# Sixteen third steps instead of twelve: four more quarter products split by Strassen-Winograd, and the vector work around them reordered

## The chip, the cores and the metric

The kernel runs on one core of a Trainium2 chip. The metric is the device time of one execution in microseconds (us); the median of several runs is given. A profiled execution of the kernel before gives a trace: instructions of each engine with start and duration, the semaphore waits between them, and the DMA transfers. Engines are named as in the profile: PE (TensorE matmuls), PEld (its weight loads), DVE (VectorE), ACT (ScalarE), POOL (GpSimd) and SP (SyncE). A name such as L463 is line 463 of the kernel.

## The reference

Two layers act on `x` of 8 sequences x 256 tokens x 1024 features, in fp32. The first adds a dense product and a gated LoRA term; the second adds a product with one of 16 whole weight matrices, chosen per sequence.

```python
def layer0(x, language_ids, W, Wr, A, B):        # W 1024x1024, 8 experts of rank 16
    base = jnp.einsum('btd,od->bto', x, W)
    logits = jnp.einsum('btd,ed->bte', x, Wr)
    logits = logits + (one_hot(language_ids, 8) * 5.0)[:, None, :]
    topw, topi = jax.lax.top_k(logits, 2)
    weights = softmax(topw)
    gates = jnp.sum(one_hot(topi, 8) * weights[..., None], axis=-2)
    h = jnp.einsum('btd,erd->bter', x, A)
    return base + 2.0 * jnp.einsum('bter,bte,eor->bto', h, gates, B)

def layer1(x, adapter_ids, weight):              # weight 16x1024x1024
    return jnp.einsum('bsi,boi->bso', x, weight[adapter_ids])

x = x + layer0(x, itok_B_0_7, W, Wr, A, B)
x = x + layer1(x, itok_B_0_15, weight)
```

## The kernel before, in words

**The first layer** is one 1024 x 1024 x 2048 product, done by Strassen-Winograd steps. The identity is added to W's diagonal (`add_identity`), so that the residual comes with the product. The first step cuts weights, inputs and outputs in two each way: blocks `w11` to `w22`, `x11` to `x22`, `y11` to `y22`. It leaves seven block products, called 1, 2, 5, 6, 3, 7 and 4 in the order in which they run. Product 1 is written out in `opening`; the others are calls of `product`. Sums of blocks that a product needs are made by VectorE (`w_sum`: S1, S2, S3, S4) or by DMAs that add to what they find (`add_x`, `add_raw` on POOL's queue, after plain loads by `raw` on SP's).

**The second step** cuts each block product into seven leaves of 256 x 256 x 512: `make_subs` makes the sums s1 to s4 of weights and t1 to t4 of inputs. In the profile's names a leaf adds into a PSUM pair A, X or B; `roles` hands the three pairs round from product to product. A plain leaf is four matmuls with a 512-wide moving operand (`mm`, L551). A matmul in fp32 stands in the trace as two records, and in the products `up` and `hg` add the LoRA rows as further matmuls.

**The third step** cuts a leaf again, into seven pieces of 128 x 128 x 256. `third` gives the eight small sums (r1 to r4 of weights, 128 wide, and q1 to q4 of inputs, 256 wide), `piece(n)` the matmul of piece n (L463), and `take(n)` its eviction. Pieces 1, 6 and 7 add into one bank one after another, with an eviction in between; piece 5 has a bank of its own; pieces 2, 3 and 4 add into the leaf's pair. So piece 6 waits for the evictions of piece 1, and piece 7 for those of piece 6. In the kernel before, twelve leaves have a third step: leaves 3 and 4 of product 1 (in `opening`), leaf 2 of products 2, 5, 6, 3, 7 and 4, leaves 3 and 4 of product 5, and leaf 4 of products 3 and 4.

**The order of VectorE's work** is set by a small planner while the program is written out. `queue` holds pending operations, each with a cost, the events it needs and a key; `now` counts estimated PE and DVE time. `ahead` writes out queued operations that are free before TensorE's time, `force(key)` writes out what a matmul is about to need, and `after` an eviction. `us(n)` is the cost of an operation on n elements. `opening` is written out by hand.

**The gates**: `project` multiplies x by A and Wr together (136 columns a token tile, L256), `take(j, c)` splits logits from h, `gating(j)` makes the top-2 gates with some twenty small operations on VectorE and multiplies them onto h, and `turn(j, banks)` transposes h on TensorE (L326), from where ScalarE copies it to `hg`. j is the half of the tokens.

**The second layer** (`adapt`, matmuls at L863, the last at L930) takes one sequence at a time with one Winograd step; `load_w1` brings its weights, `prep_w1` and `prep_y` make its sums.

Of the kernel before, what the change touches and what calls it, by code (L numbers as in the profile page):

```python
# [25 lines left out]
def kernel(  # L26
# [31 lines left out]
    nc = tc.nc  # L58
# [171 lines left out]
    def add(out_, x, y):  # L230
        tt(out_, x, y, ALU.add)
# [58 lines left out]
    def gating(j):  # L290
# [29 lines left out]
        ]  # L320
        return [(0.23, f) for f in ops] + [(1.22, onto_h)]

# [24 lines left out]
    queue = []  # L347
    done = {}

    def us(n):  # L350
        return (n + 151) / 960

    def vec(t, fn, key=None):
        fn()
        now["dve"] += t
        done[key] = now["dve"]

# [7 lines left out]
    def ahead(until):  # L365

        while now["dve"] < until:
            may = [(t, i) for i, t in enumerate(map(free, queue)) if t is not None and t < until]
            ready = [i for t, i in may if t <= now["dve"]]
            if ready:  # L370
                t, _, key, fn = queue.pop(ready[0])
                vec(t, fn, key)
            elif may:
                now["dve"] = min(may)[0]
            else:
                return
# [35 lines left out]
    def third(key, leaf, lhs, rhs, place, what):  # L412
# [10 lines left out]
        def op(name, tag, fn, x, y, what):  # L423
            width = P if name[0] == "r" else NQ

            def run():
                if place == 0:
                    t[name] = sub3.tile([P, width], F32, name=f"{name}_{key}{leaf}", tag=tag)
                else:
# [18 lines left out]

        def piece(n, acc=None, banks=None):
            if n in (1, 5):  # L450
# [11 lines left out]
            }[n]()  # L462
            nc.tensor.matmul(out_, lhsT=l, rhs=r, start=(n in (1, 5)), stop=True, skip_group_check=True)  # L463
            now["pe"] += 0.432
# [13 lines left out]

    def make_subs(key, w, x, leaves=(), what=(), last=(), place=0):

# [58 lines left out]
    def multiply(up=None, tokens=None):  # L539


        def mm(acc, lhs, rhs, first=False, rows=None, c=0, part=(0, 1), ms=(0, 1), need=()):
            if rows == "d":
                force("bdiff")
            for key in need:
# [17 lines left out]
    def opening(key, dest):  # L563
# [23 lines left out]
        for f in sums_of[:4]:  # L587
            f()
        add(dest[:, 0], A, dest[:, 0])
        wide = pair("ids_wide", 0)[:, 0, :NB]  # L590
        nc.tensor.matmul(wide, lhsT=ones, rhs=ids_f[:, :NB], start=True, stop=True)
# [8 lines left out]
        event(f"{key}:P6")  # L600
        project(0, 0, None, range(KH, KC), False)
        take(0, 0)

        late[0][3]()
        ops, ops3, piece, out = third(key, 3, lambda: t["s2"], lambda: b(1, 1), 0, ())
        for o in ops:
            vec(o[0], o[3], o[2])
        late[1][3]()
        mm(A, t["s3"], t["t3"])
# [3 lines left out]
        q1, q2 = dest[:, 1], dest[:, 2]  # L613
        chunk(0)
# [6 lines left out]
        piece(6)  # L621
        out(6, q1, q1)
        chunk(2)
        for n in (2, 3, 4):
# [4 lines left out]
        last_out = out  # L629
        ops, ops3, piece, out = third(key, 4, lambda: a(1, 1), lambda: t["t2"], 0, ())  # L630
        for o in ops[:2]:
            vec(o[0], o[3], o[2])
        last_out(5, q1, q1)
        for o in ops[2:]:
            vec(o[0], o[3], o[2])
        add(q1, B, q1)
        chunk(4)
        piece(1)
        out(1, q2)
        chunk(5)  # L640
        piece(5)
# [8 lines left out]
        piece(7)  # L650
        out(7, q2)
        out(5, q2, q2)
        add(q2, A, q2)

    def product(key, base, dest, lora=None, tokens=None, sub=False, joined=None):

# [61 lines left out]
        if 4 in deep:  # L718
            _, _, piece4, take4 = deep[4]
            piece4(1)  # L720
            take4(1, at[2], old[2], sub)
        if 3 in deep:
            _, _, piece, take = deep[3]
            force(f"{key}.X2")
# [12 lines left out]
            for n in (2, 3, 4):  # L737
                piece(n, B)
            if 4 in deep:
                force(f"{key}.A7")  # L740
                mm(A, None, None, False, "1", 0, part=())
            piece(7)
            take(7, at[1], at[1], sub)
            take(5, at[1], at[1], sub)
        else:
# [3 lines left out]
        if 4 in deep:  # L749
            if 3 not in deep:  # L750
                piece4(5)
                piece4(6)
                take4(6, at[2], old[2], sub)
                force(f"{key}.A7")
                mm(A, None, None, False, "1", 0, part=())
# [9 lines left out]
        join(2)  # L765
        ahead(now["pe"])


# [218 lines left out]
    done.clear()  # L987
    now["pe"], now["dve"] = 0.0, 3.5
    after(0.4, lambda: take(0, 1))
# [3 lines left out]
    now["pe"] += 7.5  # L993
    subs2 = make_subs("2", "12", "21", (2,))
    run(subs2[:2])
# [15 lines left out]
    gates = queue[-1][2]  # L1011
    queue += [(0.69, (), "I22", lambda: add_identity(wb["22"]))]
    queue += w_sum(minus, "21", "22", "21", (), "S1")
    queue += [(2.0, (), "bdiff", b_differences)]
# [4 lines left out]
    now["pe"] += 2.0  # L1019
# [8 lines left out]
    queue += w_sum(minus, "12", "11", "12", (), "S4")  # L1028
    queue += make_subs("3", "12", "12", (2, 4), ("x22",), "6", 1)
# [10 lines left out]
    queue += [(t, ("w0",), f"w0_{i}", f) for i, (t, _, f) in enumerate(prep_w1(0, 0))]  # L1040
    y0 = []
# [4 lines left out]

    queue += [(0.69, ("4:P7", "7:join2"), f"y0_{i}", lambda i=i: prep_y0(i)) for i in range(4)]
# [60 lines left out]
```

## Time and profile before

| what | value |
|---|---|
| median of 3 runs | 426.36 us (425.69 to 426.7) |
| the profiled execution's own time | 425.69 us |
| its span, first to last instruction | 423.7 us |
| PE, DVE, ACT busy | 418.8, 287.6, 40.6 us |
| first matmul of the opening, of product 2, of the second layer | 4.17, 59.25, 227.75 us |
| granted TensorE clock, mean | 1.00 |
| DMA traffic | 72.61 MB, mean 171 GB/s |

The span leaves out 2.0 us that lie around it in the device time. Matmuls overlap in the trace, so a matmul's cost in the queue is read from the starts of neighbours, not from its own duration: a 512-wide record lasts 592 ns and the next starts after 429. The same holds for VectorE: an operation on 1024 elements lasts 1.22 us and the next can start after 1.13. A group of rows merged in the timeline has the start of the first and the time to the end of the last.

### The profile page before, as it was taken

What the parts mean: (1) busy time and instruction counts of PE and PEld (TensorE: products, weight loads), DVE (VectorE), ACT (ScalarE), POOL (GpSimd) and SP (SyncE); (2) the same over time, 40 slices, a digit from 0 to 9 for tenths busy, and PEclk for the clock granted to TensorE, in tenths of its full rate; (3) what the DMA queues carried; (4) which work ended last, traced back from release to release, by engine and by line L of the source; (5) the groups of instructions that cost most, each with busy time, mean ns of one, the idle gap of its engine ahead of it and who ended that gap; (6) DMA issues with size and microseconds to landing.
All of it is one profiled execution on the core that took longest, in us unless ns stands there. A gap on an engine that the chain in (4) does not pass through costs nothing.

```text
span 423.7 us, 3569 instructions
## 1 busy us (share of the span) xinstructions
PE 418.8 (99%) x1294; PEld 226.1 (53%) x1294; DVE 287.6 (68%) x439; ACT 40.6 (10%) x69; POOL 17.6 (4%) x26
## 2 busy tenths in 40 slices
PE   8999999999999999999999999999999999999996
PEld 6579975445655454554555444444444444444574
DVE  1645699957888989878786666765747666665531
ACT  2010120022110000000000101010101101010110
POOL 1000020110001101103000000000000000000000
PEclk9999999999999999999999999999999999999999
DMA  8995089476220964918902384666658385650202
GB/s 274 385 397 236 2 173 210 126 184 101 100 99 4 179 215 78 294 24 155 342 0 99 116 321 159 242 214 213 224 194 300 109 298 190 213 183 0 101 0 99
DMA packets 20257, 72.61 MB, mean 171 GB/s; under 512 B 1552, under 2 KB 3856, under 8 KB 15248
## 3 DMA queue, kind: packets, MB, share of 16 engines
q1 hardware_dynamic: 15088, 58.87, 38.0%
q0 software_dynamic: 3904, 12.58, 16.6%
q10 hardware_dynamic: 1248, 0.93, 0.7%
q8 instruction: 10, 0.16, 0.1%
q14 instruction: 7, 0.06, 0.0%
HBM read 55.61 MB, written 8.39 MB: 151 GB/s over the span
## 4 chain that ended last, share of the span: by engine, by line
PE 99%; POOL 0%; ACT 0%; issue 0%; POOLq 0%
PE A L863 23%; PE A L551 21%; PE B L551 13%; PE B L863 13%; PE ps_h L256 7%; PE X L863 6%; PE P L463 5%; PE A_last L930 3%; PE X L551 3%; PE X L463 2%; PE A L463 1%; PE idle L568 1%; PE B L463 1%; PE ps_g L326 0%; ACT z L960 0%
## 5 line engine op out<-in xcount | busy, mean ns | idle before, releaser
L551 PE MATMUL A<-t,s 128*128 128x512 f32 x112 | 50.3, 592 | 0.0
L863 PE MATMUL B<-x,x 128*128 128x512 f32 x96 | 43.2, 592 | 0.0
L863 PE MATMUL A<-w,x 128*128 128x512 f32 x88 | 39.6, 592 | 0.0
L228 DVE TENSOR_TENSOR w<-w,w 128x1024 f32<-128x1024 f32 x24 | 29.1, 1223 | 15.1 <-PE A L863 15.1
L863 PE MATMUL A<-w,y 128*128 128x512 f32 x88 | 39.1, 592 | 0.0
L256 PEld LDWEIGHTS ps_h<-y,x 128*128 128x128 f32 x256 | 31.7, 190 | 3.3 <-issue 2.9
L551 PEld LDWEIGHTS A<-t,s 128*128 128x128 f32 x112 | 21.2, 190 | 21.2 <-issue 20.6
L256 PE MATMUL ps_h<-y,x 128*128 128x136 f32 x256 | 31.9, 279 | 0.0
L863 PEld LDWEIGHTS B<-x,x 128*128 128x128 f32 x96 | 18.2, 190 | 22.1 <-issue 22.0
L863 PEld LDWEIGHTS A<-w,x 128*128 128x128 f32 x88 | 16.7, 190 | 21.0 <-issue 21.0
L863 PEld LDWEIGHTS A<-w,y 128*128 128x128 f32 x88 | 16.7, 190 | 20.6 <-issue 20.6
L228 DVE TENSOR_TENSOR y<-P,y 128x512 f32<-128x512 f32 (+1 forms) x31 | 17.6, 567 | 14.0 <-PE P L463 9.1
L228 DVE TENSOR_TENSOR y<-A,y 128x1024 f32<-128x1024 f32 x17 | 20.8, 1223 | 8.3 <-issue 4.6
L551 PE MATMUL A<-x,w 128*128 128x512 f32 x56 | 25.4, 594 | 0.0
L551 PE MATMUL B<-x,s 128*128 128x512 f32 x40 | 18.0, 592 | 0.0
L228 DVE TENSOR_TENSOR x<-w,x 128x1024 f32<-128x1024 f32 (+1 forms) x11 | 10.6, 968 | 10.8 <-PE A L863 7.8
L225 ACT ACTIVATE z<-A 128x512 f32<-128x512 f32 x12 | 7.2, 597 | 101.4 <-PE A L863 101.4
L228 DVE TENSOR_TENSOR w<-x,w 128x1024 f32<-128x1024 f32 x8 | 9.7, 1225 | 10.2 <-PE A L863 5.7
L551 PEld LDWEIGHTS A<-x,w 128*128 128x128 f32 x56 | 10.3, 190 | 10.8 <-issue 10.5
L228 DVE TENSOR_TENSOR z<-z,X 128x512 f32<-128x512 f32 x7 | 4.8, 687 | 15.9 <-PE X L863 15.9
L551 PE MATMUL B<-t,s 128*128 128x512 f32 x32 | 15.0, 595 | 0.0
L863 PE MATMUL X<-w,y 128*128 128x512 f32 x32 | 14.4, 592 | 0.0
(179 smaller groups left out, 555.8 us busy)
## 6 DMA issues: line engine op xcount, KB each, us to landing
x<-w_dram SPq DMA_DIRECT2D x24, 1024.0 KB, 5.1
x<-xT_dram SPq DMA_DIRECT2D x10, 1024.0 KB, 10.6
w<-w_dram SPq DMA_DIRECT2D x8, 1024.0 KB, 4.8
out_dram<-z SPq DMA_DIRECT2D x15, 512.0 KB, 3.0
x<-x POOLq DMA_DIRECT2D x4, 1024.0 KB, 9.9
x<-xT_dram POOLq DMA_DIRECT2D x4, 1024.0 KB, 9.3
y<-y POOLq DMA_DIRECT2D x8, 512.0 KB, 5.3
w<-wT_dram SPq DMA_DIRECT2D x3, 1024.0 KB, 15.3
```

What stands on the lines that cost most here:

```text
L225: nc.scalar.activation(out_, x, AF.Copy, scale=scale)
L228: nc.vector.tensor_tensor(out_, x, y, op)
L256: nc.tensor.matmul(ps[v][:, u * EA : (u + 1) * EA], lhsT=xk(k, j, c)[:, ts(r, P)], rhs=aw_sb[:, k, :], start=(first and k == some[0] and u ...
L463: nc.tensor.matmul(out_, lhsT=l, rhs=r, start=(n in (1, 5)), stop=True, skip_group_check=True)
L551: nc.tensor.matmul(acc[:, m, :], lhsT=l, rhs=r, start=(first and i < len(ms)), stop=(i >= len(steps) - len(ms)), skip_group_check=True,)
L568: nc.tensor.matmul(idle[:, 0, :P], lhsT=ident, rhs=ident, start=True, stop=True)
L863: nc.tensor.matmul(accs[name], lhsT=lhs[:, k // 2, k % 2, :], rhs=rhs[:, k, :], start=(first and k == 0), stop=(k == KH - 1), skip_group_c ...
L930: nc.tensor.matmul(acc, lhsT=lhs[:, k // 2, k % 2, :], rhs=rhs[:, k, ts(v, m)], start=(first and k == 0), stop=(k == KH - 1), skip_group_c ...
```

## The change

Four more leaves get a third step: leaf 5 of product 1, leaf 4 of products 2 and 6, and leaf 3 of product 4.

- In `opening` the leaf s1 x t1 is cut. Its result is needed in two quarters of y21, q3 and q1. ScalarE copies pieces 1, 6 and 7 into both (`both`), VectorE adds piece 5 to both, and pieces 2 to 4 (P3's sums) are held in B. B is added to q3, then leaf 3's pieces 2 to 4 are added into B as well, and B is added to q1. `add_B` leaves out the quarter that no piece writes. A after s2 x t2, copied by ScalarE before, is added to q1 by VectorE. The sums of leaves 3 and 4 are made one leaf earlier, and some go into free space of y12 (`place == 3`).
- w22's identity, the weight sum S1 and the differences of B's rows (`b_differences`) move from the planner's queue in product 2 to the end of the opening.
- The second half's transposes move from after product 2 to within it (`between=turn_1`), into pair X.
- In `product`, leaf 4's pieces 5 and 6 stand between the halves of B where leaf 3 is not cut; where it is, leaf 3's last piece and evictions come before A's LoRA rows. While leaves 3 and 4 are under way, `hold` keeps the planner to operations whose key begins with the product's number.
- S4 enters the queue before product 5 and no longer before product 3. The planner's costs change. At the start of the second layer pairs X and B swap roles.

The diff, cut to its core:

```diff
     def us(n):
-        return (n + 151) / 960
+        return (n + 66) / 960
     def vec(t, fn, key=None):
         fn()
         now["dve"] += t
-        done[key] = now["dve"]
+        done[key] = now["dve"] + 0.1
     def ahead(until):
         while now["dve"] < until:
-            may = [(t, i) for i, t in enumerate(map(free, queue)) if t is not None and t < until]
+            may = [
+                (t, i)
+                for i, t in enumerate(map(free, queue))
+                if t is not None and t < until and queue[i][2][0] in (hold[0] or queue[i][2][0])
+            ]
...
         if 4 in leaves:
-            deep[4] = third(key, 4, lambda: a(1, 1), lambda: t["t2"], 2, (f"{key}:P6",))
+            deep[4] = third(key, 4, lambda: a(1, 1), lambda: t["t2"], 3 if early else 2, (f"{key}:P6",))
...
     def opening(key, dest):
...
         for f in sums_of[:4]:
             f()
+        ops, ops3, piece, out = third(key, 5, lambda: t["s1"], lambda: t["t1"], 0, ())
+        for o in ops[:2]:
+            vec(o[0], o[3], o[2])
         add(dest[:, 0], A, dest[:, 0])
...
+        own = halves(pair(f"P5_{key}", 0))
         B = pair(f"B_{key}", 2)
-        mm(B, t["s1"], t["t1"], True)
-        nc.scalar.copy(dest[:, 3], B)
+        def both(n):
+            out(n, q3)
+            out(n, q1)
+        def add_B(q):
+            for m, n in ((0, 2 * NQ), (1, NQ)):
+                add(q[:, m, :n], B[:, m, :n], q[:, m, :n])
+        piece(1, banks=own)
+        piece(5, banks=own)
+        both(1)
+        mm(A, t["s2"], t["t2"])
...
+        piece(6)
+        both(6)
+        for n in (2, 3, 4):
+            piece(n, B, fresh=True)
+        project(0, 0, None, (KH,), False, False)
+        piece(7)
+        both(7)
+        add(q1, A, q1)
+        for q in (q3, q1):
+            out(5, q, q)
+        add_B(q3)
+        project(0, 0, None, range(KH + 1, KC), False)
+        take(0, 0)
-        mm(A, t["s2"], t["t2"])
-        nc.scalar.copy(dest[:, 1], A)
...
         piece(7)
         out(7, q2)
+        add_identity(wb["22"])
+        for f in w_sum(minus, "21", "22", "21"):
+            f[3]()
+        b_differences()
         out(5, q2, q2)
         add(q2, A, q2)
...
-    def product(key, base, dest, lora=None, tokens=None, sub=False, joined=None):
+    def product(key, base, dest, lora=None, tokens=None, sub=False, joined=None, between=None):
...
+        if between is not None:
+            between(X)
         if 3 in deep:
+            hold[0] = key
...
+        elif 4 in deep:
+            mm(B, t["s2"], b(1, 1), False, "d", 1, ms=(0,), need=K("s4", "B5"))
+            piece4(5)
+            mm(B, t["s2"], b(1, 1), False, "d", 1, ms=(1,))
+            piece4(6)
+            take4(6, at[2], old[2], sub)
...
-    subs2 = make_subs("2", "12", "21", (2,))
+    subs2 = make_subs("2", "12", "21", (2, 4), early=True)
...
-    product("2", y21, y11, 0, 0)
-    force(gates)
-    turn(1, singles("ps_g_1"))
+    def turn_1(X):
+        force(gates)
+        turn(1, halves(X))
+        now["pe"] += 1.8
+    product("2", y21, y11, 0, 0, between=turn_1)
...
-    queue += make_subs("6", "11", "22", (2,), ("T2",), "5", 0)
+    queue += make_subs("6", "11", "22", (2, 4), ("T2",), "5", 0)
+    queue += w_sum(minus, "12", "11", "12", (), "S4")
     product("5", None, y22, 1, 1)
...
-    queue += make_subs("4", "22", "22", (2, 4), ("T4",), "7", 1)
+    queue += make_subs("4", "22", "22", (2, 3, 4), ("T4",), "7", 1)
...
+    role[1:] = role[2], role[1]
     for u in range(NB):
```

More of the change, by code (lines that the diff above doesn't have):

```diff
@@ L320, in gating @@
         ]
-        return [(0.23, f) for f in ops] + [(1.22, onto_h)]
+        return [(0.26, f) for f in ops] + [(us(2 * TQ), onto_h)]
     def turn(j, banks):
@@ L348 @@
     done = {}
+    hold = [""]
     def us(n):
-        return (n + 151) / 960
+        return (n + 66) / 960
     def vec(t, fn, key=None):
@@ L428, in run @@
                     t[name] = sub3.tile([P, width], F32, name=f"{name}_{key}{leaf}", tag=tag)
+                elif place == 3:
+                    t[name] = flat(yb["12"])[:, 2048 + at[tag] : 2048 + at[tag] + width]
                 else:
@@ L447, in third, with piece @@
         ]
-        def piece(n, acc=None, banks=None):
+        def piece(n, acc=None, banks=None, fresh=False):
             if n in (1, 5):
@@ L462, in piece @@
             }[n]()
-            nc.tensor.matmul(out_, lhsT=l, rhs=r, start=(n in (1, 5)), stop=True, skip_group_check=True)
+            nc.tensor.matmul(out_, lhsT=l, rhs=r, start=(n in (1, 5) or fresh and n in (2, 4)), stop=True, skip_group_check=True)
             now["pe"] += 0.432
@@ L477, in third, with make_subs @@
         return ops, ops3, piece, take
-    def make_subs(key, w, x, leaves=(), what=(), last=(), place=0):
+    def make_subs(key, w, x, leaves=(), what=(), last=(), place=0, early=False):
         before = (f"{last}:P7",) if last else ()
@@ L542, in mm @@
         def mm(acc, lhs, rhs, first=False, rows=None, c=0, part=(0, 1), ms=(0, 1), need=()):
-            if rows == "d":
-                force("bdiff")
             for key in need:
@@ L588, in opening @@
             f()
+        q1, q2, q3 = (dest[:, q] for q in (1, 2, 3))
+        ops, ops3, piece, out = third(key, 5, lambda: t["s1"], lambda: t["t1"], 0, ())
+        for o in ops[:2]:
+            vec(o[0], o[3], o[2])
         add(dest[:, 0], A, dest[:, 0])
-        wide = pair("ids_wide", 0)[:, 0, :NB]
+        wide = pair("ids_wide", 2)[:, 0, :NB]
         nc.tensor.matmul(wide, lhsT=ones, rhs=ids_f[:, :NB], start=True, stop=True)
         use_ids(wide)
+        own = halves(pair(f"P5_{key}", 0))
         B = pair(f"B_{key}", 2)
-        mm(B, t["s1"], t["t1"], True)
-        nc.scalar.copy(dest[:, 3], B)
+        def both(n):
[8 more added lines that the diff above has]
+        mm(A, t["s2"], t["t2"])
+        event(f"{key}:P6")
+        for o in ops[2:]:
+            vec(o[0], o[3], o[2])
         for f in sums_of[4:]:
             f()
-        mm(A, t["s2"], t["t2"])
-        nc.scalar.copy(dest[:, 1], A)
-        event(f"{key}:P6")
-        project(0, 0, None, range(KH, KC), False)
-        take(0, 0)
+        for o in ops3:
+            vec(o[0], o[3], o[2])
         late[0][3]()
-        ops, ops3, piece, out = third(key, 3, lambda: t["s2"], lambda: b(1, 1), 0, ())
-        for o in ops:
+        next_leaf = third(key, 3, lambda: t["s2"], lambda: b(1, 1), 3, ())
+        for o in next_leaf[0]:
             vec(o[0], o[3], o[2])
         late[1][3]()
+        piece(6)
[11 more added lines that the diff above has]
+        take(0, 0)
+        ops, ops3, piece, out = next_leaf
         mm(A, t["s3"], t["t3"])
@@ L612, in opening @@
         chunk = lambda k: project(0, 1, quarter, (k,), k == 0, k == KC - 1)
-        q1, q2 = dest[:, 1], dest[:, 2]
         chunk(0)
@@ L622, in opening @@
         out(6, q1, q1)
+        next_leaf = third(key, 4, lambda: a(1, 1), lambda: t["t2"], 0, ())
+        for o in next_leaf[0]:
+            vec(o[0], o[3], o[2])
         chunk(2)
@@ L629, in opening @@
         last_out = out
-        ops, ops3, piece, out = third(key, 4, lambda: a(1, 1), lambda: t["t2"], 0, ())
-        for o in ops[:2]:
-            vec(o[0], o[3], o[2])
+        ops, ops3, piece, out = next_leaf
         last_out(5, q1, q1)
-        for o in ops[2:]:
-            vec(o[0], o[3], o[2])
-        add(q1, B, q1)
+        add_B(q1)
         chunk(4)
+        chunk(5)
         piece(1)
         out(1, q2)
-        chunk(5)
         piece(5)
@@ L738, in product @@
                 piece(n, B)
+            piece(7)
+            take(7, at[1], at[1], sub)
+            take(5, at[1], at[1], sub)
             if 4 in deep:
@@ L741, in product @@
                 mm(A, None, None, False, "1", 0, part=())
-            piece(7)
-            take(7, at[1], at[1], sub)
-            take(5, at[1], at[1], sub)
+        elif 4 in deep:
[4 more added lines that the diff above has]
+            take4(6, at[2], old[2], sub)
         else:
@@ L750, in product @@
             if 3 not in deep:
-                piece4(5)
-                piece4(6)
-                take4(6, at[2], old[2], sub)
                 force(f"{key}.A7")
@@ L765, in product @@
         join(2)
+        hold[0] = ""
         ahead(now["pe"])
@@ L987 @@
     done.clear()
-    now["pe"], now["dve"] = 0.0, 3.5
+    now["pe"], now["dve"] = 0.0, 6.0
     after(0.4, lambda: take(0, 1))
@@ L1011 @@
     gates = queue[-1][2]
-    queue += [(0.69, (), "I22", lambda: add_identity(wb["22"]))]
-    queue += w_sum(minus, "21", "22", "21", (), "S1")
-    queue += [(2.0, (), "bdiff", b_differences)]
     queue += make_subs("5", "21", "12", (2, 3, 4), ("T1",), "2", 1)
-    product("2", y21, y11, 0, 0)
-    force(gates)
-    turn(1, singles("ps_g_1"))
-    now["pe"] += 2.0
+    def turn_1(X):
[3 more added lines that the diff above has]
+    product("2", y21, y11, 0, 0, between=turn_1)
     raw("21", 0, 1)
@@ L1027 @@
     event("x22", 14.0)
-    queue += w_sum(minus, "12", "11", "12", (), "S4")
     queue += make_subs("3", "12", "12", (2, 4), ("x22",), "6", 1)
@@ L1037 @@
     event("w0", 18.0)
-    queue += make_subs("4", "22", "22", (2, 4), ("T4",), "7", 1)
+    queue += make_subs("4", "22", "22", (2, 3, 4), ("T4",), "7", 1)
     product("7", y21, y21, joined=(y22, y21))
-    queue += [(t, ("w0",), f"w0_{i}", f) for i, (t, _, f) in enumerate(prep_w1(0, 0))]
+    queue += [(t, ("w0",), f"4.w{i}", f) for i, (t, _, f) in enumerate(prep_w1(0, 0))]
     y0 = []
@@ L1045, in prep_y0 @@
         y0[i][2]()
-    queue += [(0.69, ("4:P7", "7:join2"), f"y0_{i}", lambda i=i: prep_y0(i)) for i in range(4)]
+    queue += [(0.6, ("4:P7", "7:join2"), f"4.y{i}", lambda i=i: prep_y0(i)) for i in range(4)]
     product("4", y21, y21, 1, 0)
```

## The prediction

> **What bounds the kernel now.** I read the page's span and busy rows first, then its chain, then what TensorE waited for, then busy times by stage, then timelines around the edits.
>
> ```profile
> span 423.7 us, 3569 instructions
> PE 418.8 (99%) x1294; PEld 226.1 (53%) x1294; DVE 287.6 (68%) x439; ACT 40.6 (10%) x69; POOL 17.6 (4%) x26
> PE 99%; POOL 0%; ACT 0%; issue 0%; POOLq 0%
> ```
>
> TensorE is busy from 1.4 us to the end, and the chain that ended last is TensorE alone. Its only recorded wait is at the start:
>
> ```profile
> PE idle L568 <- POOL ident masks.py:199: 1.4, 1, 1.4
> ```
>
> So whatever is taken from TensorE's queue shortens the span one for one, as long as no operand or bank comes late. The stage view says where that could happen (columns: stretch, its length, then busy time of PE, PEld, DVE, ACT, POOL, the clock, DMA):
>
> ```profile
> 15.90:30.00 14.10, 14.10 (x58) 8.36 (x58) 5.62 (x15) 2.77 (x4) 0.00 (x0) 1.00 1.06 392
> 59.20:89.90 30.70, 30.70 (x82) 14.98 (x81) 27.97 (x56) 2.92 (x6) 3.00 (x3) 1.00 0.86 181
> 120.30:144.10 23.80, 23.80 (x64) 11.96 (x64) 21.22 (x26) 1.58 (x2) 2.56 (x2) 1.00 0.32 49
> 144.10:174.20 30.10, 30.10 (x86) 15.98 (x85) 26.27 (x44) 1.00 (x1) 2.61 (x3) 1.00 0.68 177
> 198.00:227.90 29.90, 29.90 (x85) 15.92 (x84) 22.57 (x34) 1.00 (x1) 0.86 (x1) 1.00 0.56 176
> ```
>
> These are the opening's middle, and products 2, 6, 3 and 4. TensorE fills each. VectorE has 8.5 us free in the first and 2.7, 2.6, 3.8 and 7.3 us in the others: it is the engine that more work could turn into a bound.
>
> **What the Trainium skill says.** "TensorE: Matmul & The Clock Gate", Step-by-step: what each phase is for, says that weights are loaded ahead of matmuls still in flight. The trace agrees: 226 us of loads, no idle TensorE. It also shows the exception, a bank that comes free just as its turn comes:
>
> ```profile
> 36.70 1.09 PE L256 MATMUL ps_h<-y,x 128*128 128x136 f32 x8
> 37.65 0.70 PE L463 MATMUL P<-t,w 128*128 128x256 f32 x2
> 38.18 1.09 PE L256 MATMUL ps_h<-y,x 128*128 128x136 f32 x8
> ```
>
> VectorE's last read of that bank (36.90 plus 0.69) ended at 37.59. The two records took 0.53 us to the next start; elsewhere 0.43. So a just-in-time release costs 0.10 us without showing as idle. "VectorE: DVE Perf Modes", The perf-mode tier table (the rule you actually need), lists a two-tensor fp32 operation at 1× alone, from SBUF or PSUM; the trace agrees, with starts 1.135 us apart for 1024 elements, 0.60 for 512, 0.34 for 256 and 0.205 for 128. I use these steps below.
>
> **The change part by part.** *Four leaves get a third step*: P5 of the first product (opening), leaf 4 of products 2 and 6, leaf 3 of product 4. A leaf was four 512-wide matmuls, eight records of 0.429 us: 3.43 us (A at 120.28 to 123.78, less its 0.07 of late release). Split, it is seven 256-wide ones, 14 records of 0.216: 3.02 us (three in a row started at 34.05, 34.48, 34.91). The changed program's order confirms the count: 372 matmuls of 512 for 388, 144 of 256 for 116. TensorE: 4 x (3.02 - 3.43) = **-1.63 us**, all on the path.
>
> *VectorE pays.* Each leaf needs four 128-wide and four 256-wide sums, 4 x 0.205 + 4 x 0.34 = 2.18 us, and in a product four more evictions, 2 x 0.34 + 2 x 0.60 = 1.88: 4.06 us in each of products 2, 6 and 4. In the opening there are 2.18 of sums, 1.13 for A (ScalarE copied it), 2 x 0.60 for P5's halves, 0.94 for the held sums into q3, and 0.2 saved on q1: 5.3 us. ScalarE there swaps two 1.01 us copies for four of 0.37 and two of 0.59. None is on the path if each leaf's operands are early. I laid the changed order of each queue out with the durations above; four places come within 0.3 us:
>
> (a) *Opening, A for P6.* The sum y<-A must have read A before t2·s2 is added. Before, P5's 3.43 us stood between; now only pieces 1 and 5.
>
> ```profile
> 13.68 1.22 DVE L228 TENSOR_TENSOR t<-x,t 128x1024 f32<-128x1024 f32 x1
> 14.82 1.22 DVE L228 TENSOR_TENSOR y<-A,y 128x1024 f32<-128x1024 f32 x1
> ```
>
> ```profile
> 15.55 0.38 PE L591 MATMUL ids_wide<-ids_f,ones 1*128 1x8 f32 x2
> 15.86 3.70 PE L551 MATMUL B<-t,s 128*128 128x512 f32 x8
> ```
>
> VectorE now does r1 and q1 first: y<-A from 14.82 + 0.55 = 15.37 to 16.59. TensorE arrives at 15.86 + 0.86 = 16.72: 0.13 us to spare. (b) *Opening, A for P7.* TensorE: 16.72, A 3.43, piece 6 0.43, pieces 2 to 4 1.29, one chunk 0.93, piece 7 0.43, three chunks 2.78: at 26.0. Piece 7's result is there at 23.4; two ScalarE copies (the pair at 59.45 took 1.07) to 24.5, y<-A to 25.75: 0.25 to spare. (c) *Product 6, piece 7 of leaf 4.* From the end of P7: TensorE needs 1, half of B, 5, half of B, 6, 2 to 4, that is 6 x 0.43 + 2 x 1.72 = 6.02 us. VectorE: r1, q1 0.5, A7 1.13, P1 0.34, four sums 1.09, product 3's s 0.60, r3 and q3 0.55, its t 1.13, then P6's eviction to 5.8: 0.2 to spare. (d) *Product 4, leaf 3's piece 5*: A7 and two evictions of P1 end 2.4 us after P7; TensorE has 0.43 + 0.43 + 1.72 = 2.58: 0.2 to spare. Each costs 0 to 0.10 us when met as at 37.65, and what it is late when late. I take 0.15 for all, less the just-in-time releases of before, 0.10 at 37.65 and 0.07 at 120.28, whose order changes: -0.02, ends -0.17 and +0.8.
>
> *Moves that I cost at nothing.* The second gates' eight transposes (0.87 us, at 89.74 before) now stand within product 2, in bank X: the same count; their gates ended at 66.9, X is read out at 79.5, and ScalarE's two copies (1.1 us) have until the first use at 96.20. w22's identity, S1 and the b differences (0.60 + 2 x 1.135 + 1.6 = 4.5 us) leave product 2, which makes room for its 4.06, and go into the opening's hole, where VectorE waited 2.90 us for ScalarE until 44.37. They wait for w21, which landed at 39.6 (issued 22.3, 17.3 to landing), some 0.7 us ahead; behind them stand leaf 4's last evictions and the second half's gating, whose banks TensorE needs near 50: some 5 us of cover. S4 (2.3 us) moves from product 3 (148.46) into products 5 and 6: that makes room for what product 6 pushes out. SP's second x21 load (83.07) waits some 3 us longer for leaf 4's operands, and the load and POOL's add behind it with it; product 7 first reads them near 174. The planner's changed costs, the hold, and the swapped banks of the second layer only order the queues; no PSUM bank is added.
>
> Sum: -1.63 - 0.02, about **-1.6 us**. Against the profiled execution's own 425.69 us (span 423.7 and 2.0 around it) that gives 424.1. The median shown is 426.36, 0.67 above; I carry the difference over: 424.8. About 0.2% (0.85 us) is what a measurement of this kernel can tell from no change.
>
> **Rivals.**
> 1. *The gain is given back in waits (no change).* The places (a) to (d) miss: 0.2 to 0.5 us each, about 1.2 in all, -0.4 net: 426.0. For: spare times of 0.13 to 0.25 us. Against: they are differences of rows that repeat within 0.01 us. Chance 0.12.
> 2. *VectorE becomes the bound in products 6 and 3 (slower).* From 120.3 to 174.2 it was busy 47.5 of 53.9 us; with 4.06 more and S4's 2.3 gone it has 49.3, 91%. If chained small sums run longer than those of before, or TensorE's evictions queue behind them, product 3's s and t, which in my layout are 0.7 us early at its B (147.84 before), come late, and each product behind inherits it. It decides from 0.7 us of added VectorE delay on; at the whole 4.06 less 0.7, 3.4 us is lost: 428.1. Against: after product 7, VectorE has 4.0 us free. Chance 0.08.
> 3. *It doesn't do what it says*: 256-wide pieces cost over half a 512. The rows exclude it (0.432 against 0.858), and it is in the sum.
>
> **How the numbers follow.** My forecast, 424.8 us, chance 0.80: faster by over 0.2%. Rival 1 gives within 0.2% (0.12), rival 2 slower (0.08). The range starts 0.8 below, for the runs' scatter (425.69 to 426.7), and reaches to 426.4, taking in the bound of +0.8 and rival 1; rival 2 is left out.
>
> **What would show each step.** After: PE busy near 417.2, 1318 records, the chain still TensorE alone; seven P and B starts 0.43 apart in the opening where B took 3.70; A at 16.7 and 26.0 with no idle before it; product 2's first A at 58.8 instead of 59.25; the second layer's first matmul near 226.1 instead of 227.75; VectorE near 305 us. Wrong: TensorE idle named <-DVE at A in the opening or at B or P in products 6, 3, 4, or a second layer that starts later than 227.

## The result, and the profile after

The changed kernel takes **424.38 us** (median of 20 runs, 423.75 to 425.23), the kernel before, run beside it, 426.01 us (20 runs, 425.08 to 426.74). The ratio is 0.9964, with a 95% interval of 0.9958 to 0.9970: 1.63 us or 0.36% less, beyond the 0.2% that the prediction took as the least that can be told from no change. The forecast was 424.8 us.

The page of the profile after, its span, its busy times and its chain:

```profile
span 422.2 us, 3674 instructions
PE 417.1 (99%) x1318; PEld 230.7 (55%) x1318; DVE 304.8 (72%) x489; ACT 40.9 (10%) x73; POOL 17.6 (4%) x26
PE 99%; POOL 0%; ACT 0%; issue 0%; POOLq 0%
```

TensorE has 24 records more (1318 for 1294) and is busy 1.7 us less; VectorE is busy 17.2 us more; the chain is still TensorE alone. In the waits of TensorE there is again only the start:

```profile
PE idle L573 <- POOL ident masks.py:199: 1.4, 1, 1.4
```

The stages that the prediction showed, in the windows of the profile after (same columns: stretch, its length, then PE, PEld, DVE, ACT, POOL, clock, DMA), in the order opening, product 2, product 6, product 3, product 4:

```profile
15.90:30.00 14.10, 14.10 (x67) 9.88 (x67) 11.65 (x27) 3.01 (x8) 0.00 (x0) 1.00 1.06 391
...
58.80:89.50 30.70, 30.70 (x93) 16.59 (x92) 26.61 (x59) 4.01 (x8) 3.00 (x3) 1.00 0.87 184
...
119.30:142.40 23.10, 23.10 (x69) 12.84 (x68) 21.37 (x36) 1.58 (x2) 2.56 (x2) 1.00 0.27 50
142.40:172.60 30.20, 30.20 (x86) 16.06 (x86) 30.06 (x51) 1.00 (x1) 2.34 (x3) 1.00 0.67 169
...
196.20:226.10 29.90, 29.90 (x92) 17.18 (x91) 26.74 (x46) 1.00 (x1) 0.89 (x2) 1.00 0.58 178
```

TensorE fills every stretch. The surprise is the fourth line: in product 3 VectorE is busy 30.06 of 30.20 us, 99.5%, and yet TensorE doesn't wait.

**A finer ruler.** The time to the `ids_wide` row in the opening differs by up to 1.25 us between profiled executions (it starts between 15.29 and 16.54 us). Behind it the traces repeat closely: three executions of kernels without a late TensorE (the one above, e9 and e11 below) agree within 0.01 us. So from here on kernels are compared by their *length*: from the start of `ids_wide` to the end of the last matmul. Before: 15.55 to 420.26, **404.71 us**. After: 15.65 to 418.53, **402.88 us**. That is 1.83 us less. The medians show 1.63 of it; where the rest may lie is said at the end, under the median.

### The profile page after: what moved, and what is told of

The parts are those of the page before. It is cut to its first block, busy times and chain, and to the rows that moved or that the text cites. A ratio compares the mean times of both kernels' runs of the same rounds, so it can differ in the third digit from the quotient of the medians.

```text
span 422.2 us, 3674 instructions
## 1 busy us (share of the span) xinstructions
PE 417.1 (99%) x1318; PEld 230.7 (55%) x1318; DVE 304.8 (72%) x489; ACT 40.9 (10%) x73; POOL 17.6 (4%) x26
## 4 chain that ended last, share of the span: by engine, by line
PE 99%; POOL 0%; ACT 0%; issue 0%; POOLq 0%
PE A L908 23%; PE A L556 20%; PE B L908 13%; PE B L556 11%; PE ps_h L256 7%; PE X L908 7%; PE P L470 6%; PE A_last L975 3%; PE X L470 3%; PE X L556 3%; PE A L470 2%; PE B L470 1%; PE idle L573 1%; PE X L326 0%; PE ps_g L326 0%; ACT z L1005 0%
## 5 line engine op out<-in xcount | busy, mean ns | idle before, releaser
L228 DVE TENSOR_TENSOR y<-A,y 128x1024 f32<-128x1024 f32 x18 | 22.0, 1222 | 9.3 <-PE A L556 5.8
L228 DVE TENSOR_TENSOR y<-P,y 128x512 f32<-128x512 f32 (+1 forms) x37 | 21.1, 572 | 8.0 <-PE P L470 6.2
L556 PE MATMUL B<-x,s 128*128 128x512 f32 x32 | 14.9, 592 | 0.0
L228 DVE TENSOR_TENSOR x<-x 128x1024 f32<-128x1024 f32 (+1 forms) x15 | 14.7, 1005 | 0.0
L720 ACT COPY X<-A 128x1024 f32<-128x1024 f32 x6 | 6.0, 997 | 89.8 <-PE A L556 89.8
```

The source lines that it names most:

```text
L228: nc.vector.tensor_tensor(out_, x, y, op)
L556: nc.tensor.matmul(acc[:, m, :], lhsT=l, rhs=r, start=(first and i < len(ms)), stop=(i >= len(steps) - len(ms)), skip_group_check=True,)
L720: nc.scalar.copy(X, A)
```

## The experiments

Three explanations stood beside each other, in short (each expectation gives them in numbers). COUNT: the time follows TensorE's own queue steps, and the moved vector work gains nothing by itself. ORDER: the moves themselves shorten the time. VECTORE: cut leaves alone make TensorE wait for VectorE, so that the moves are what lets the leaves pay. What was measured (each ratio is to runs of the kernel before that were made beside it, medians 425.91 to 426.09 us in the experiments; e9 and e10 are single runs, read by their traces alone):

| kernel | median us (runs) | ratio to before, 95% interval | length us | beside after |
|---|---|---|---|---|
| before | 426.01 (20) | 1 | 404.71 | +1.83 |
| after | 424.38 (20) | 0.9964 (0.9958 to 0.9970) | 402.88 | 0 |
| e1 moves only | 426.31 (13) | 1.0008 (1.0000 to 1.0016) | 405.02 | +2.14 |
| e2 opening only | 425.66 (13) | 0.9996 (0.9987 to 1.0004) | 404.47 | +1.59 |
| e3 leaves only | 431.86 (4) | 1.0147 (1.0127 to 1.0167) | 410.60 | +7.72 |
| e4 S1 back | 426.29 (21) | 1.0008 (1.0001 to 1.0015) | 404.68 | +1.80 |
| e5 turn back | 425.75 (20) | 0.9996 (0.9988 to 1.0004) | 404.17 | +1.29 |
| e6 seventeen | 424.20 (6) | 0.9957 (0.9941 to 0.9972) | 402.56 | -0.32 |
| e7 seventeen, GpSimd | 426.74 (19) | 1.0019 (1.0011 to 1.0028) | 405.22 | +2.34 |
| e8 twenty sums | 432.32 (2) | 1.0153 (1.0127 to 1.0180) | 410.39 | +7.51 |
| e9 four sums | 425.00 (1) | none | 402.87 | -0.01 |
| e10 six sums | 424.81 (1) | none | 403.93 | +1.05 |
| e11 after again | 424.75 (6) | 0.9962 (0.9948 to 0.9976) | 402.87 | -0.01 |
| e12 seventeen, halves | 423.65 (5) | 0.9939 (0.9925 to 0.9953) | 402.55 | -0.33 |

**e1: the moves without the leaves.** The opening keeps its plain leaf, and the three `make_subs` lists are as before; the planner, the earlier S1 and b differences, and the second turn within product 2 are as after.

```diff
-    subs2 = make_subs("2", "12", "21", (2, 4), early=True)
+    subs2 = make_subs("2", "12", "21", (2,))
...
-    queue += make_subs("6", "11", "22", (2, 4), ("T2",), "5", 0)
+    queue += make_subs("6", "11", "22", (2,), ("T2",), "5", 0)
...
-    queue += make_subs("4", "22", "22", (2, 3, 4), ("T4",), "7", 1)
+    queue += make_subs("4", "22", "22", (2, 4), ("T4",), "7", 1)
```

> The changed kernel with its four new third steps taken out again (opening written as before, leaf 4 of products 2 and 6 and leaf 3 of product 4 plain) but with the moves kept: S1, w22's identity and the b differences at the end of the opening, the second turn within product 2, S4 early, hold, the new planner costs, the swapped banks. Theory COUNT (the gain is TensorE's shorter queue, 0.41 us a leaf): +1.64 us on the changed kernel, so level with the kernel before, ratio 1.000 within 0.001, TensorE's last matmul near 420.2 us. Theory ORDER (the gain is from the moves and from bank releases that no longer come just in time): it keeps half or more of the gain, ratio 0.998 or less.

Measured: 405.02 us of length, 0.31 more than before. TensorE is late once where before was not, at the first piece of product 2 (its timeline):

```profile
62.84 0.70 PE L470 MATMUL P<-x,w 128*128 128x256 f32 x2
```

The piece starts 0.27 us late, its second record another 0.10: the first of ScalarE's two copies of `ps_h` ran from 62.42 to about 62.8, behind VectorE's sums of `ps_h` and `bias` at 62.22. Less the 0.07 that before lost at 120.28, that is the 0.31. The moves alone gain nothing: ORDER falls. (The opening's own reordering is not among them, since it comes with its leaf.)

**e2: only the opening's leaf is cut,** with all the moves; the three `make_subs` lists are those of e1.

> The changed kernel with only the opening's new third step (P5 of product 1); the three new leaves of products 2, 6 and 4 are plain again, the moves are kept. COUNT: one leaf, 0.41 us under the kernel before, ratio 0.999, TensorE's first matmul of product 2 at 58.8 as in the changed kernel, its last near 419.8. ORDER: as e1, no different from it. If the opening's extra evictions cost anything, product 2 starts later than 58.9.

Measured: 404.47 us, 0.24 less than before. In this execution place (a) of the prediction was missed (VectorE's, then TensorE's timeline):

```profile
12.44 1.23 DVE L228 TENSOR_TENSOR t<-x 128x1024 f32<-128x1024 f32 x1 [0.53 <-DMA x<-xT_dram]
...
15.86 1.22 DVE L228 TENSOR_TENSOR y<-A,y 128x1024 f32<-128x1024 f32 x1
```

```profile
17.13 1.12 PE L556 MATMUL A<-t,s 128*128 128x512 f32 x2
```

The sum that frees A ended at 17.08, and A started 0.27 us late, plus 0.10 on its second record. What came late was the load of x (t at 12.44, in the profile after at 12.07). The sum fits: one leaf, -0.41, +0.37 for the wait, -0.17 for the two small losses of before that are gone, together -0.21. So this run doesn't show a cost of the opening's leaf itself, but that its place (a) can be missed.

**e3: the leaves without the moves.** Products 2, 6 and 4 get their leaves, the planner, S1, the b differences and the second turn are as before, and so is the opening.

```diff
-    product("2", y21, y11, 0, 0, between=turn_1)
+    queue += [(0.69, (), "I22", lambda: add_identity(wb["22"]))]
+    queue += w_sum(minus, "21", "22", "21", (), "S1")
+    queue += [(2.0, (), "bdiff", b_differences)]
...
+    product("2", y21, y11, 0, 0)
+    force(gates)
+    turn(1, singles("ps_g_1"))
```

> The kernel before with only the three new leaves of products 2, 6 and 4 (no third step for P5, no moves, old planner costs, no hold). If VectorE's added work is hidden wherever it stands (COUNT alone): three leaves, -1.23 us, ratio 0.997. Theory VECTORE (the leaves pay only because the moves make room on VectorE): product 2 has 27.97 + 4.06 = 32.0 us of VectorE work for 30.3 us of TensorE, product 6 21.2 + 4.06 for 23.4; TensorE waits 1.7 us or more in product 2 and some in 6 and 3; slower than the kernel before, by 1 to 5 us, ratio 1.002 to 1.012, with idle TensorE named after DVE.

Measured: slower than before by 5.9 us. TensorE's waits, and its timeline at the end of product 2:

```profile
PE ps_g L326 <- DVE y L228: 2.2, 1, 2.2
...
PE P L463 <- DVE y L228: 1.4, 1, 1.4
```

```profile
90.29 0.70 PE L463 MATMUL P<-y 128*128 128x256 f32 x2 [1.36 <-DVE y L228]
93.16 1.84 PE L326 MATMUL ps_g<-ident,y 128*128 128x128 f32 x8 [2.18 <-DVE y L228]
94.80 3.77 PE L551 MATMUL A<-x,w 128*128 128x512 f32 x6
```

Piece 7 of leaf 4 waits for the leaf's own small sums (the last one that it reads ends at 90.23), and the transposes for the evictions of their bank, which VectorE starts only at 92.42: 3.97 us with the late second record. What follows runs slowly: the eight transposes need 1.64 us instead of 0.87, and the first records of A are 0.85 us apart instead of 0.43 (94.80, 95.65, 96.50), another 1.8 us. Smaller waits, in product 3 and the second layer above all, bring 1.4. With three leaves' -1.22 the sum is 5.95. VECTORE holds: the leaves alone lose, the moves alone gain nothing, both together gain 1.8. Two of the moves are taken out one at a time in e4 and e5. The planner's costs, `hold`, the earlier S4 and the new order of leaf 4's pieces are also missing in e3; no run changes one of these alone, so their shares stay open.

**e4: S1 and the b differences back in product 2's queue,** all else as after.

```diff
-        add_identity(wb["22"])
-        for f in w_sum(minus, "21", "22", "21"):
-            f[3]()
-        b_differences()
...
+    queue += [(0.6, (), "I22", lambda: add_identity(wb["22"]))]
+    queue += w_sum(minus, "21", "22", "21", (), "S1")
+    queue += [(1.6, (), "bdiff", b_differences)]
```

> The changed kernel with one move undone: w22's identity, S1 and the b differences (4.5 us of VectorE) go back from the opening's end to the queue of product 2. COUNT alone: no change, ratio to the kernel before 0.9965. VECTORE: product 2 has 26.6 + 4.5 = 31.1 us of VectorE work for 30.7 of TensorE, and B's rows wait for the b differences; 0.5 to 3 us are lost against the changed kernel, so ratio 0.998 to 1.003, with TensorE waiting for DVE at B in product 2 (about 82 us).

Measured: the whole gain is gone, 404.68 us. TensorE's waits:

```profile
PE B L558 <- DVE bdiff L228: 1.1, 1, 1.1
PE B L558 <- DVE y L228: 0.2, 1, 0.2
```

The first of them in TensorE's timeline:

```profile
83.86 1.13 PE L558 MATMUL B<-hg,bdiff 128*128 128x512 f32 x2 [1.07 <-DVE bdiff L228]
```

B with the b differences starts 1.23 us late at 83.86, its second record 0.10 more; another B at 95.95, in product 5, costs 0.47. Their sum, 1.80, is what the length grew by.

**e5: the second turn back behind product 2.**

```diff
-    product("2", y21, y11, 0, 0, between=turn_1)
+    product("2", y21, y11, 0, 0)
+    force(gates)
+    turn(1, singles("ps_g_1"))
+    now["pe"] += 2.0
```

> The changed kernel with the second half's eight transposes put back after product 2, into the banks P1 and P5, as before. My prediction costed this move at nothing. If that holds in the changed kernel too: no difference, ratio to the kernel before 0.9965. Theory VECTORE: product 2 now ends with leaf 4's pieces in the same two banks, and the transposes wait until VectorE has read pieces 7 and 5 (two evictions, 0.69 and 0.69 us, after the last piece at 89.3): 1.0 to 2.5 us of TensorE waiting for DVE at the transposes near 90 us, ratio 0.999 to 1.002.

Measured: +1.29 us. The waits show one line more than after (TensorE's timeline below it):

```profile
PE ps_g L326 <- DVE y L228: 0.8, 1, 0.8
```

```profile
90.23 1.38 PE L326 MATMUL ps_g<-ident,y 128*128 128x128 f32 x8 [0.78 <-DVE y L228]
```

The transposes need a bank that leaf 4's last two evictions read, the first of them from 89.48 to about 90.16; at 90.23 they start 0.95 us late and take 1.22 us until the next A instead of 0.87, together 1.30.

**e6: a seventeenth leaf,** leaf 4 of product 7: what the same mechanism would still give.

```diff
-    queue += make_subs("7", "21", "21", (2,), ("T3",), "3", 0)
+    queue += make_subs("7", "21", "21", (2, 4), ("T3",), "3", 0)
```

> The changed kernel with a seventeenth third step, leaf 4 of product 7. COUNT alone: another -0.41 us, ratio to the kernel before 0.9955, TensorE's last matmul near 418.1. VECTORE: products 3, 7 and 4 have 30.1 + 19.5 + 26.7 = 76.3 us of VectorE work for 83.7 of TensorE and 4.06 more to do; what product 7 leaves over meets the first sequence's weight sums (5.9 us) at product 4's start, and place (d), 0.27 us to spare in the changed kernel, is passed: TensorE waits some 0.4 us or more at leaf 3's piece 5 near 219 and the gain is gone, ratio 0.9955 to 0.998.

Measured: -0.32 us. Of the leaf's -0.41, 0.06 is given back at X at 219.53 (place (d)), which comes just as VectorE frees it, and 0.04 at 222.61. So COUNT was nearly right, and VECTORE's wait of 0.4 us didn't come. The medians are too coarse for this: the intervals of e6 and of the changed kernel overlap.

**e7: the seventeenth leaf, with four 1024-wide sums for the second layer on GpSimd** instead of VectorE.

```diff
-        nc.vector.tensor_tensor(out_, x, y, op)
+        eng[0].tensor_tensor(out_, x, y, op)
...
+    prep = prep_w1(0, 0)
+    queue += [(t, ("w0",), f"4.w{i}", f) for i, (t, _, f) in enumerate(prep[:2])]
+    queue += [(0.05, ("w0",), f"4.p{i}", lambda f=f: on_pool(f)) for i, (_, _, f) in enumerate(prep[2:])]
```

> As e6, and the four large sums of the first sequence's weights (4.5 us of VectorE at the start of product 4) are done by GpSimd, which has nothing to do there. VECTORE: with that room the seventeenth leaf pays its full -0.41 us: TensorE's last matmul near 418.1, no wait near 219, ratio 0.9955. Against it: GpSimd is slow on these or slows VectorE beside it, so that the second layer's second or third matmul group (after 229 us) waits for it; then ratio 0.997 or more. If it reaches 0.9955 it is the fastest version here.

Measured: +2.34 us instead of a relief. GpSimd's and VectorE's timelines, and the first two of these VectorE sums in the profile after:

```profile
201.89 5.02 POOL L230 TENSOR_TENSOR x<-x,w 128x1024 f32<-128x1024 f32 x2 [0.81 <-DVE w L230]
206.87 5.30 POOL L230 TENSOR_TENSOR w<-x 128x1024 f32<-128x1024 f32 x2
```

```profile
203.35 1.35 DVE L230 TENSOR_TENSOR r<-w 128x128 f32<-128x128 f32 x1 [1.01 <-PE P L477]
204.62 2.56 DVE L230 TENSOR_TENSOR q<-x 128x256 f32<-128x256 f32 x1
207.11 1.21 DVE L230 TENSOR_TENSOR y<-A,y 128x1024 f32<-128x1024 f32 x1
...
208.57 1.38 DVE L230 TENSOR_TENSOR s<-w,s 128x512 f32<-128x512 f32 x1
209.99 2.32 DVE L230 TENSOR_TENSOR x<-s 128x128 f32<-128x128 f32 x1
```

```profile
203.77 0.28 DVE L228 TENSOR_TENSOR r<-w 128x128 f32<-128x128 f32 x1
203.97 0.42 DVE L228 TENSOR_TENSOR q<-x 128x256 f32<-128x256 f32 x1
```

While GpSimd works, VectorE's small sums from two tiles of the state buffer take 1.35, 2.56 and 2.32 us where they take 0.28 and 0.42 in the profile after, and the 512-wide one 1.38 instead of 0.68. Each of them ends 0.2 to 0.6 us after a GpSimd sum does (these end at 204.54, 206.89, 209.39 and 212.15). The sums with one operand in PSUM keep their time (y<-A,y its 1.21, y<-P,y 0.41). VectorE falls behind by that: y<-B,y starts at 212.78 for 209.86 after, 2.6 us later when the 0.35 us by which `ids_wide` is later in e7 is taken off. TensorE then waits at 216.85, 218.84 and 221.71 (the longest is shown), with the late second records 2.76 us; less the leaf, 2.35.

```profile
218.84 0.70 PE L477 MATMUL X<-x,s 128*128 128x256 f32 x2 [1.29 <-DVE y L230]
```

**e8: twenty useless sums on VectorE in product 6,** behind y<-y,B near the end of product 6, to load rival 2's place until it gives way.

```diff
+            if key == "6":
+                for _ in range(20):
+                    add(scratch, ident, ident)
```

> The changed kernel with 20 more 128-wide VectorE sums (4.1 us, their result is used by nothing) in product 6 ahead of leaf 4's last evictions. It measures rival 2 of the prediction: from which VectorE delay on TensorE waits, and whether the time comes back. In the changed kernel's trace the tightest operand behind that place is 0.9 us early. Rival 2 as stated: 4.1 less 0.9, about 3.2 us of waiting in product 3, not given back, so 3 to 3.5 us slower than the changed kernel. If VectorE had real room (COUNT): under 1 us. A waiting TensorE may also run slower for a while after.

Measured: +7.51 us. VectorE's timeline, and TensorE's:

```profile
142.92 6.49 DVE L229 TENSOR_TENSOR scratch<-ident 128x128 f32<-128x128 f32 x20
```

```profile
150.06 1.22 PE L471 MATMUL P<-x,w 128*128 128x256 f32 x2 [3.79 <-DVE y L229]
152.04 3.78 PE L557 MATMUL B<-x 128*128 128x512 f32 x4 [0.75 <-DVE y L229]
```

Since all twenty write one tile, they step by 0.325 us, not 0.205, so the delay was 6.4 us and not the 4.1 it was laid out for. TensorE is late by about 5.1 us of it, and runs at half its pace in between and behind it (four records of B in 3.78 us for 1.88), another 2.4 us. None of it comes back later. Rival 2's mechanism is real, and the 3 to 3.5 us expected were too few for two reasons: the delay was longer, and the slow stretch came on top.

**e9: four useless sums ahead of y<-A in the opening,** place (a).

```diff
+            for _ in range(4):
+                add(scratch, ident, ident)
             add(dest[:, 0], A, dest[:, 0])
```

> The changed kernel with four sums of two 128 x 128 tiles more on VectorE ahead of y<-A in the opening (work of no use, into a tile of its own). Such sums, which all write one tile, stepped by 0.325 us in the run with twenty of them, so y<-A comes 1.3 us later. SPARE (place (a) has the 0.23 us that the changed kernel's trace shows, and what is late beyond it is lost for good): TensorE waits near 1.07 us at A at 16.94, and from the ids_wide row to the last matmul it takes 402.88 + 1.1 to 1.2 = 404.0 to 404.1 us. BUFFERED (TensorE has other work in its queue or the gap is made up by later work): under 403.2 us. KNOCK-ON (the opening's later places, (b) above all, miss as well): over 404.6 us.

Measured: 402.87 us, no loss. The expected 404.0 is missed. VectorE's timeline, then TensorE's:

```profile
15.26 1.26 DVE L229 TENSOR_TENSOR scratch<-ident 128x128 f32<-128x128 f32 x4
16.44 1.22 DVE L229 TENSOR_TENSOR y<-A,y 128x1024 f32<-128x1024 f32 x1
```

```profile
17.82 1.02 PE L557 MATMUL A<-t,s 128*128 128x512 f32 x2
```

In this execution `ids_wide` came at 16.54, 0.9 us later than in the profile after, and VectorE did not. So y<-A, though delayed, was done at 17.66 and A started in time. Nothing was late, so e9 says nothing on what a late A costs. It shows that the spare of the profile after is no fixed number. There y<-A ends at 16.71 and A starts at 16.94, 0.23 us later (VectorE's timeline, then TensorE's):

```profile
15.49 1.22 DVE L228 TENSOR_TENSOR y<-A,y 128x1024 f32<-128x1024 f32 x1
```

```profile
16.94 3.60 PE L556 MATMUL A<-t,s 128*128 128x512 f32 x8
```

In eight of the other executions with the cut opening leaf (e4 to e8 and e10 to e12) the spare at (a) was 0.74 to 0.81 us, in the profile after 0.23, in e2 it was missed by 0.27. About 0.8 is the most it can be, since y<-A must wait for TensorE's earlier matmuls into A (in e4 for 0.45 us). From their end in e9, at 15.69, y<-A would have started at about 15.8 without the four sums (an estimate: in e4 it starts 0.11 us behind them). So of the 1.3 us only some 0.6 delayed it, and the spare of 0.8 swallowed that.

**e10: six useless sums instead of twenty in product 6,** below and above the spare that the profile after shows.

> The changed kernel with six sums of two 128 x 128 tiles more on VectorE in product 6, where the run before this had twenty. At 0.325 us each they delay VectorE by 1.95 us. THRESHOLD (VectorE, 99.5% busy in product 3, is just under the bound: the tightest operand there is 0.96 us early, and only what goes beyond it is lost): waits of about 1.0 us in product 3, 0.1 more for late releases, length 403.9 to 404.1 us instead of 402.88. BOUND (VectorE already sets the pace in products 6 and 3, all of the 1.95 us is lost): 404.8 us or more. SLACK (product 3 has room that the trace doesn't show): under 403.3 us.

Measured: 403.93 us, +1.05. VectorE's timeline and TensorE's:

```profile
142.54 1.92 DVE L229 TENSOR_TENSOR scratch<-ident 128x128 f32<-128x128 f32 x6
144.37 1.40 DVE L229 TENSOR_TENSOR y<-y,P 128x512 f32<-128x512 f32 x2
145.80 1.22 DVE L229 TENSOR_TENSOR y<-y,A 128x1024 f32<-128x1024 f32 x1
```

```profile
147.08 1.98 PE L557 MATMUL B<-x 128*128 128x512 f32 x4 [0.76 <-DVE y L229]
```

The sums delay VectorE by 1.83 us (142.54 to 144.37); B starts 0.92 us late and its second record 0.10 more. What was swallowed is 1.83 - 0.92 = 0.91 us. In the profile after the same place shows it directly, VectorE's timeline and TensorE's:

```profile
144.34 1.22 DVE L228 TENSOR_TENSOR y<-y,A 128x1024 f32<-128x1024 f32 x1
```

```profile
146.52 1.88 PE L556 MATMUL B<-x 128*128 128x512 f32 x4
```

y<-y,A ends at 145.56, and B starts at 146.52: 0.96 us to spare. THRESHOLD holds: of a delay of VectorE that arises here, some 0.9 us is swallowed and the rest is lost. A smaller delay was not tried. One that arises ahead of place (c), some 4 us earlier, would meet the 0.36 us to spare there first.

**e11 and e12: the changed kernel again, and beside it seventeen leaves with the first y<-A in two halves,** so that A's first bank is free earlier.

```diff
-        add(dest[:, 0], A, dest[:, 0])
+        for m in range(2):
+            add(dest[:, 0, m], A[:, m], dest[:, 0, m])
...
-    queue += make_subs("7", "21", "21", (2,), ("T3",), "3", 0)
+    queue += make_subs("7", "21", "21", (2, 4), ("T3",), "3", 0)
```

> The changed kernel itself, to stand beside the next one on the same chip: 0.996 of the time before, 402.9 us from the ids_wide row to the last matmul.

> Seventeen third steps (leaf 4 of product 7 too), and the first y<-A of the opening in two halves, so that A's first bank comes free 0.5 us sooner and place (a) has 0.7 us to spare instead of 0.23. COUNT: -0.41 us for the leaf, +0.06 to 0.1 for the late X that seventeen showed at 219.5; the halves gain nothing in a run where place (a) is met anyway and 0.2 to 0.4 us in one where x's load lands late: 0.3 to 0.5 us under the changed kernel, 402.5 us of length. FULL (VectorE near product 4 has no room left for one leaf more): within 0.1 us of the changed kernel or above it.

Measured: e11 repeats the result (0.9962; length 402.87). e12 is the fastest of all, 423.65 us, 0.9939 of before, with TensorE busy 416.6 us and VectorE 308.7. Of the 1.1 us between the two medians its length explains 0.32: the leaf's -0.41 and 0.05 and 0.04 us of late X at 218.56 and 221.63. The profiled executions differ by 1.38: beside the 0.32, 0.87 lies ahead of `ids_wide` (15.50 against 16.37), where the edit changes nothing, and 0.19 behind the last matmul. Why all five runs of e12 lie below all six of e11 is not explained. Place (a) was met in both, and e12's length is that of e6, which has the same leaves without the halves (402.56), so what the halves are worth wasn't seen.

## Why the prediction was right, point by point

- **The leaves, -1.63 us.** Right. 1318 records came as counted, and the length fell by 1.83 = 1.63 + 0.10 + 0.07 and a rest of 0.03. The other marks agree more closely than they had to: PE busy is 417.1 for the 417.2 expected, product 2's first A is at 58.83 (58.8), the second layer starts at 226.02 (226.1). These take in the uneven start, and that it was alike in the two profiled executions is luck: e11, the same kernel, is 0.7 us later and has PE busy 417.8.
- **Just-in-time releases, -0.02.** This term of the sum was mis-sized. The 0.17 of before (37.65 and 120.28) went, and none of the allowed +0.15 came: -0.17. Behind `ids_wide` only one second record is late in the profile after, at 16.29, and its counterpart is late before too. The ends given, -0.17 and +0.8, held it.
- **The four close places.** All four were met in the profile after, (a) with 0.23 us for 0.13, (b) with 0.24 for 0.25, (c) with 0.36 for 0.2, (d) with 0.27 for 0.2. Rival 1 did not come about there. For (a) that is in part luck: its spare is no property of the program alone. e2 missed it through a late load of x, and most profiled executions had 0.8 to spare. How often the other runs miss it is not known. The argument against rival 1, that rows repeat within 0.01 us, is true within the products and not for the opening, where loads and TensorE's first steps shift against each other.
- **"Moves that I cost at nothing."** In their own cost that is right within 0.3 us (e1). But the text took the leaves' gain as if the moves were a side matter, and only named the room they make. e4 and e5 price them: with the leaves in place, the S1 move is worth 1.80 us and the turn 1.29. Either one left out takes most of the gain or nearly all of it.
- **S4 "from product 3 (148.46) into products 5 and 6": wrong.** This step failed. Before, S4 was queued ahead of product 6, not of product 3 as the text of the change has it, and S3 ahead of product 3. So the pair at 148.46 was S3 (w21), which stayed in product 3 (151.43 in the profile after); S4 ran at 125.34 and 127.11 in product 6 before, and runs at 125.67 and 127.35, still in product 6, after. It only enters the queue earlier. VectorE's timeline before, then after:

```profile
125.34 1.22 DVE L228 TENSOR_TENSOR w<-w,w 128x1024 f32<-128x1024 f32 x1
127.11 1.22 DVE L228 TENSOR_TENSOR w<-w,w 128x1024 f32<-128x1024 f32 x1
...
148.46 2.35 DVE L228 TENSOR_TENSOR w<-w,w 128x1024 f32<-128x1024 f32 x2
```

```profile
125.67 1.22 DVE L228 TENSOR_TENSOR w<-w,w 128x1024 f32<-128x1024 f32 x1
127.35 1.22 DVE L228 TENSOR_TENSOR w<-w,w 128x1024 f32<-128x1024 f32 x1
...
151.43 2.35 DVE L228 TENSOR_TENSOR w<-w,w 128x1024 f32<-128x1024 f32 x2
```

  So product 3 got no relief, and VectorE's 49.3 of 53.9 us in products 6 and 3 should have read 47.5 + 4.06 = 51.6; the windows show 21.37 + 30.06 = 51.43 of 53.3 us, 96.5% instead of 91%.
- **Rival 2** was closer than its 0.08 said. Its stage and mechanism were right (e8, e10), its point of decision 0.9 us instead of 0.7. But the tightest operand at product 3's B is not the s and t that it named: in the profile after, the t that this B reads is done at 141.52, 5.0 us ahead of it, and the last thing it needs is the bank that y<-y,A reads until 145.56. What saved the change was not the 4.6 us of room that the prediction counted in products 6 and 3, for only 1.9 were left: VectorE's results came in the right order, each a little ahead of its reader. Its price, delay less spare, was too low for long delays: in e8 2.4 us of slow matmuls came on top.
- **VectorE +17.5 us**: 17.2 measured, and off the path as argued; ScalarE's swap came to +0.3 us. The second x21 load was held up by 2.2 us (it is issued at 85.24, before at 83.07), near the 3 us expected, but the add behind it on POOL's queue was not: the load landed in 7.1 us instead of 10.0, and the add starts at 92.89 (93.67 before).
- **The median.** The profiled execution plus its 2.0 gave 424.1, and 424.8 came from carrying the 0.67 between profile and median over. The 20 runs gave 424.38; the first three runs of before had been high (426.36 against 426.01 in 20). The miss of 0.4 us is mostly these 0.35 and the 0.15 of the releases. Part of the length's gain does not show in the time: what lies around the span is 2.15 us in the profiled executions with the opening's new leaf (1.75 in e7), and 2.00 in before, e1 and e3, which lack it. The prediction carried the 2.0 over; why it grew by 0.15 is open.

## What to carry to other kernels

Where one engine sets the end without a gap, count its queue steps, and then ask for each stage what makes room for the work that the saving puts on other engines: here the cut of four leaves gained 1.8 us only with moves that by themselves gain nothing. A helper engine that is 99% busy is no bound as long as each result is ready before its reader; the number that decides is the smallest lead of a result over its use, and a few useless operations measure it. Before a moved step is priced by a row of the trace, make sure by its operands and its place in the queue which step that row is.

## What the runs showed of the hardware that was not expected

- **A long wait of TensorE costs more than itself.** After waits of 1.36 and 2.18 us (e3) and of 3.79 and 0.75 us (e8), 512-wide records stepped by 0.85 us instead of 0.43 for 2.3 us (e3) and 3.6 us (e8); the granted clock is 0.57 from 93 to 97 us in e3 and 0.53 from 152 to 156.2 us in e8. Waits of up to 1.3 us (e4, e5, e7, e10) had no such tail on 512-wide records. The Trainium skill, "TensorE: Matmul & The Clock Gate", What's actually happening, tells of a clock that falls to half after an idle window of some 3.4 us; e8's 3.79 us agrees with it, while e3 fell with two shorter waits and 0.5 us of work between them. The same page says that the window runs free of the kernel, so that the first matmuls' slow stretch varies. Two executions of the same changed kernel agree with that, the one of the result and e11: the second and third record of the first X step by 0.56 and 0.43 us in the one and by 0.85 each in the other, and this is where e11's `ids_wide` falls 0.7 us behind (TensorE's timelines, first X):

```profile
4.27 2.60 PE L556 MATMUL X<-x,w 128*128 128x512 f32 x4
```

```profile
4.21 3.37 PE L556 MATMUL X<-x,w 128*128 128x512 f32 x4
```

- **GpSimd's sums hold up VectorE's.** The skill's "GPSIMD Engine Reference", 1. Specifications, says that the two share their interfaces to the state buffer and contend when VectorE has two inputs there. e7 agrees and gives the size: a 128-wide sum held up to 2.32 us, about as long as GpSimd's own 2.39 to 2.80 us, while sums with one operand in PSUM kept their time.
- **Sums into one tile step slower.** Twenty 128-wide sums into the same tile were 0.325 us apart (e8), six 0.326 (e10); small sums into different tiles 0.205. These useless sums also read one and the same tile as both inputs; no run tells the two apart.
